# A graph layer on one core: another order of VectorE's operations, register loads a step ahead, and edge codes as products on TensorE

## The chip, the cores and the metric

One core of a Trainium2 chip runs the kernel. The metric is the device time of one execution in microseconds (us), lower is better. In what follows PE is TensorE (matrix products; PEld its weight loads), DVE is VectorE, ACT is ScalarE, POOL is GpSimd, and SP is the engine that issues most of the transfers. A small q behind an engine (DVEq) means its sequencer: register operations and the like, which are not counted as busy.

## The reference

There are 12500 nodes of 128 features and 400000 edges, sorted by their target `dst`. An edge's message is the source's row times one of two weight matrices, by the edge's type, plus a bias. Messages are summed by target; a third matrix is applied to the node itself; then relu, residual and a layer norm without gain:

```python
Xs = X[src]
m_data = Xs @ W_data.T + b_data
m_ctrl = Xs @ W_control.T + b_control
msg = jnp.where((edge_types == 0)[:, None], m_data, m_ctrl)
agg = jax.ops.segment_sum(msg, dst, num_segments=X.shape[0])
out = agg + (X @ W_self.T + b_self)
h = jax.nn.relu(out)
...
x = _layernorm(x + h, axis=-1)
```

## The kernel before

The sum over edges is taken first and the weights are applied after it: for each target and each type the kernel sums the rows of x, as three bf16 parts that add up to the f32 value (`x3`), and multiplies the sums by the weights afterwards. The sums run on PE: rows of messages times a 0/1 matrix which says to which target and type each edge goes.

Edges are cut into chunks of 128, and chunks into 25 groups of 125. A group has five windows of 25 chunks: 5 chunks ("p") whose rows POOL gathers from memory by indirect transfers (`msg`), and 20 chunks ("e") whose rows are fetched from a copy of x in on-chip memory by products with 0/1 matrices. In most groups the fifth window is gathered whole, so there are 109 "e" windows, and the main loop has 109 steps, `w`, one for each.

A step does several things for several windows at once. For window `w` PE picks rows (`got`, L974, with the matrix `pick`), ACT copies them to `emsg`, and PE adds them into `sums` (L803) with the 0/1 matrices `esel`, which DVE makes by comparing codes (L541, from `choose`). For the gathered chunks DVE makes `psel` (L541) in the same way. When a window is complete, DVE adds `sums` to the accumulator `acc` or `cnt` at a place known only from the data (`accumulate`, L860). That place is read from a table in on-chip memory into a register of DVE by `place_of` (`value_load`, L854), just before the addition that needs it.

For windows `w + 2` and `w + 3` DVE also works out where each edge's row lies and in which order (`give_slots`). Its operations, in short names with the page's tile names: `blocks` makes O (L541), `same` (L612), `tens` and the folds (L622, L627) add up O; PE turns these into counts (L634, in `before`); `ahead` (L642) adds them, `product` (L648) multiplies, `half` and `fourth` (L656), `eighth` (L661) and `found` (L666) reduce to a rank, `rank` (L671) copies it, `matrix` makes rm (L541), `key` (L678), `values` makes rv (L713). PE then puts the values in place (`put`, L726), ACT copies them to `cell`, SP writes them to memory and reads them back for all partitions (`spread`), and `pick_matrix` (L790) compares the result a step later. `over` and `own_before` (L686 to L701, L562, L568, L574) treat edges that found no room. The tile `prod` has one buffer, so `same` of window `w + 3` comes after `found` of `w + 2`. `sums` has two buffers.

Once for each group, `prep` turns the raw edge lists into codes: `begin`, `rows` (DVE: `rel`, `kind`, `code_r`, `worst`), `turn` (PE transposes into `side`, ACT copies), `then`. `finish_batch` (L1078 to L1124) applies the weights and the layer norm to finished rows.

What orders the work: each piece has a time within its step between 0 and 1, and `merged` sorts all pieces by that number into program order. A planner then orders each engine's queue by program order and by when it expects the operands. `after` (and `tc.issue_after`) binds an instruction to come later in the queue than another on the same engine. The list `order` in the main loop is such a chain for DVE: its pieces come one after another (`in_turn` hands each piece the instruction before it); work that is not on the list, such as the additions, `psel` and the norm, falls between where the planner puts it.

Of the kernel before, what the change touches and what calls it, by code (L numbers as in the profile page):

```python
# [8 lines left out]
FP = mybir.dt.float32  # L9
BF = mybir.dt.bfloat16  # L10
# [4 lines left out]
OP = mybir.AluOpType  # L15
# [4 lines left out]
P = 128  # L20
# [4 lines left out]
GC = 125  # L25
# [6 lines left out]
NE = 5  # L32
# [5 lines left out]
PW = DPC + 2 * PAD  # L38
EW = 86
AW = PW + DPC * (PL - 1)  # L40
WMAX = max(AW, EW)
CHUNKS = PB + EC
M0 = 50
R = 640
# [164 lines left out]
def short_path(ctx, tc, const, ident, eps, wT, brow, bad, x, src, dst, etype, ws, bs, out):  # L209
    nc = tc.nc  # L210
    keep = ctx.enter_context(tc.tile_pool(name="keep", bufs=1))
# [3 lines left out]
    pre = ctx.enter_context(tc.tile_pool(name="pre", bufs=2))  # L215
# [6 lines left out]
    def side():  # L222

        return ps1.tile([P, 512], FP, name="side")

    def windows(g):

        c = g * GC
        for i in range(NE):
            yield "p", i, c, PB  # L230
            yield "e", i, c + PB, EC
            c += PB + EC

    def sets(g):

        return NE if g % EACH == 0 else NE - 1
# [5 lines left out]
    each_e = [(g, i) for g in range(NG) for i in range(sets(g))]  # L242
    raw = {}
# [110 lines left out]
    ident_b = keep.tile([P, P], BF, name="ident_b")  # L354
# [39 lines left out]
    over_n = keep.tile([P, len(each_e)], BF, name="over_n")  # L394

    bounds_of, from_of, pick_first = row_tables(nc, keep, tmp)
    least = tmp.tile([1, NG, NWIN], FP, name="least")
    for i, (_, _, c, _) in enumerate(windows(0)):
        nc.vector.memset(least[:, :, i:i + 1], float(max(0, c * DPC - PAD)))
# [42 lines left out]
    def twice(t2, t):  # L442
        return nc.scalar.copy(t2, t.rearrange("p (n o) -> p n o", o=1).to_broadcast(list(t2.shape)))  # L443
# [35 lines left out]
    def prep(g):  # L479

        s, d, t = raw.pop(g)
        v = 0 if sets(g) == NE else 1
        width = bounds_of[:GC, v, 0:1]
        sf = pre.tile([GC, P], FP, name="sf", bufs=1)
        rel = pre.tile([GC, 2, P], BF, name="rel", bufs=1)
        code = pre.tile([GC, 2, P], FP, name="code_r", bufs=1)
        kind = pre.tile([GC, P], FP, name="kind_r", bufs=1)
        idx = pre.tile([P, GC], I32, name="idx_g", bufs=3)
        vals2 = pre.tile([P, GC, 2, 2], BF, name="vals2", bufs=3)
        near2 = pre.tile([P, GC, 2], BF, name="near2", bufs=3)  # L490

        def begin():
            nc.scalar.copy(sf, s)

        def rows():
            near = near_of(g, d)
            for k in range(2):
                nc.vector.tensor_scalar(rel[:, k], d, near[k], None, op0=OP.subtract)
            nc.vector.tensor_single_scalar(kind, t, 0.0, op=OP.not_equal)
            nc.vector.scalar_tensor_tensor(code[:, 1], kind, width, rel[:, 1], op0=OP.mult, op1=OP.add)  # L500
            nc.vector.scalar_tensor_tensor(code[:, 0], kind, float(PW), rel[:, 0], op0=OP.mult, op1=OP.add)
            for j, op in enumerate((OP.max, OP.min)):
                nc.vector.tensor_tensor(worst[:GC, v, j], worst[:GC, v, j], rel, op=op)

        def turn():
            ps = side()
            for k, each in enumerate((sf, code[:, 1], code[:, 0])):
                nc.tensor.transpose(ps[:, k * P:k * P + GC], each, ident[:GC, :GC])
            nc.scalar.copy(idx, ps[:, :GC])
            twice(vals2[:, :, 1, :], ps[:, P:P + GC])  # L510
            twice(near2, ps[:, 2 * P:2 * P + GC])

        def then():
            parts = pre.tile([P, 2, GC], I32, name="parts")
            nc.vector.tensor_single_scalar(parts[:, 0, :], idx, 7, op=OP.logical_shift_right)
            nc.vector.tensor_single_scalar(parts[:, 1, :], idx, 127, op=OP.bitwise_and)
            code_e = vals2.rearrange("p n v t -> p v t n")[:, 1, 0]
            pk = pre.tile([P, GC], FP, name="pk", bufs=3)
            nc.vector.scalar_tensor_tensor(pk, idx, 256.0, code_e, op0=OP.mult, op1=OP.add)
            blk = blks[g % 3]  # L520
            blk2 = pre.tile([P, GC, 2], BF, name="blk2", bufs=3)
            nc.scalar.copy(blk[:, :, EC:], parts[:, 0, :].rearrange("p (i c) -> p i c", c=CHUNKS)[:, :, PB:])
            twice(blk2, parts[:, 0, :])
            codes["e", g] = (blk, blk2, vals2, pk)
            codes["p", g] = (idx, near2)
            return twice(vals2[:, :, 0, :], parts[:, 1, :])

        return [begin, rows, turn, then]

    slots, placed = {}, []  # L530
    pairs = len(each_e)

    def after(ins):
        return tc.issue_after(ins.ins) if ins is not None else ExitStack()
# [252 lines left out]
    def pick_matrix(w, prev):  # L787
        t = slots[w]["pick"].rearrange("p j r -> p (j r)")
        with after(prev):
            return nc.vector.tensor_scalar(t, t, lane_f, None, op0=OP.is_equal)  # L790
# [55 lines left out]
    def acc_rows(g, a, b):  # L846
        begin_acc(g)
        return acc[g][:, a:b, :]

    def place_of(g, i):  # L850

        parts_in[g] = parts_in.get(g, 0) + 1
        with tc.issue_after(added[-2].ins) if len(added) > 1 else ExitStack():
            return nc.vector.value_load(raw["place"][0:1, g, i:i + 1], min_val=0, max_val=R - WMAX)  # L854

# [322 lines left out]
    def begin_slots(w):  # L1178
        slots[w] = give_slots(w)
        return list(slots[w]["begin"].values())  # L1180
# [25 lines left out]
    chunks, closed, rest = {}, {}, []  # L1206
# [22 lines left out]
    for w in range(pairs):  # L1229
        g, i = each_e[w]  # L1230
        more = [(0.5, lambda: later(near_rows))] if w == 0 else []
        first = 1 if g == 0 else 0
        if i == first and g + 1 < NG:
            prepared = [(at, lambda u=u: later(u)) for at, u in zip((0.15, 0.4, 0.65, 0.1), prep(g + 1))]
            more += prepared[:3]
        if i == first + 1 and g + 1 < NG:
            more += prepared[3:]
        if i == 3 and g + 2 < NG:
            load(g + 2)
        tiled, begin, chain, first = {}, [], {}, None  # L1240
        if w + 2 < pairs:
            tiled, first, chain = slots[w + 2]["tiled"], slots[w + 2]["before"], slots[w + 2]["chain"]
            begin = [(0.58, slots[w + 2]["over"])]
        elif w + 2 == pairs:
            tiled, begin = last_spares()
            first = begin.pop(0)[1]
        if w + 3 < pairs:
            more += [(0.503, lambda: begin_slots(w + 3))]
        if w + 1 == pairs:
            closes = [at for at, _ in chunks[w]][-1 - of_p(NG - 1, NE - 1)]  # L1250
            (xs, *most), (xs2, turn2, *last) = (finish(NG - 1, soon[i]) for i in (NE - 2, NE - 1))
            more += [(0.05, xs), (0.06, xs2), (0.98, turn2), (0.3, check_all)] + evenly(most, closes + 0.01, 0.97)
        units, ending, (second, third) = picked(w, tiled, ending, first)

        def started(name):
            return (lambda prev: slots[w + 3]["begin"][name](prev)) if w + 3 < pairs else None

        order = [
            (0.305, second), (0.31, chain.get("ahead")), (0.33, chain.get("product")), (0.34, chain.get("half")),
            (0.36, third), (0.38, chain.get("fourth")), (0.51, chain.get("eighth")),  # L1260
            (0.52, chain.get("found")), (0.53, started("same")), (0.54, chain.get("rank")),
            (0.55, chain.get("matrix")), (0.56, chain.get("key")), (0.57, chain.get("values")),
            (0.6, (lambda prev: pick_matrix(w + 1, prev)) if w + 1 < pairs else None),
            (0.62, started("blocks")), (0.64, started("tens")), (0.66, started("fold5")),
            (0.67, started("fold2")), (0.68, started("fold1")),
        ]
        order = [(at, f) for at, f in order if f]
        order = [(at, u) for (at, _), u in zip(order, in_turn([f for _, f in order]))]
        merged(
            chunks.pop(w, []),  # L1270
            units,
            begin,
            order,
            more,
            evenly(rest, 0.1),
        )
        slots.pop(w)
        rest = []
        for p in closed.pop(w, []):
            gp, ip = divmod(p, NE)  # L1280
            if ip == NE - 1:
                rest.append(lambda gp=gp: pass_on(gp))
                if gp < NG - 1:
                    rest += finish(gp, range(4))
                if gp + 2 < NG:
                    rest.append(lambda gp=gp: begin_acc(gp + 2))
# [143 lines left out]
```

## Time and profile before

| | before |
|---|---|
| median of 3 runs | 1719.48 us (1718.93 to 1721.28) |
| profiled execution, its own time | 1719.45 us |
| span in the profile | 1717.7 us |
| instructions | 67684 |
| granted TensorE clock, mean | 0.996 |
| DMA | 246.05 MB, mean 143 GB/s |

The span is the time from the program's first to its last instruction in the profile. The page gives busy time for each engine as a share of the span. Its chain follows the work that ended last backwards, at each step to what released it. "Issue" stands for time in which an engine waited for nothing that the profile shows. A row of the groups has line, engine, operation, output and inputs, then busy us, mean ns of one, and the idle time in front of them with what ended it.

### The profile page before, as it was taken

To read this page: it belongs to the slowest core of one execution; us is meant where nothing else is said; L and a number is where in the kernel's file an instruction comes from. 1 tells how busy PE (TensorE), PEld (TensorE's weight loads), DVE (VectorE), ACT (ScalarE), POOL (GpSimd) and SP (SyncE) were. 2 spreads that over 40 slices of the span, in tenths; PEclk is the share of its full clock that TensorE was granted. 3 is DMA by queue.
4 is the path that set the end of the run, shared out by engine and by line. 5 is a ranking of instruction groups with operands and counts; after the bars stand their busy time and mean duration, and the time that the engine had idled before them with its cause. 6 is when DMAs were issued, how large, how long until landed. Compare 5 with 4: busy or idle time off the path is not lost.

```text
span 1717.7 us, 67684 instructions
## 1 busy us (share of the span) xinstructions
PE 1554.5 (90%) x27966; PEld 1225.1 (71%) x27966; DVE 1577.5 (92%) x4078; ACT 1229.1 (72%) x2056; POOL 1217.5 (71%) x1022
## 2 busy tenths in 40 slices
PE   0699999899999999899899999999999999999998
PEld 0477777777777777777777777777777777777776
DVE  9799999999999999999999999999999999999994
ACT  7677767677767777677676777677686777677774
POOL 1377767777776777667777777677777787787682
PEclk9999999999999999999999999999999999999999
DMA  7944444444454444444444454444444454444442
GB/s 227 269 136 134 148 129 148 135 150 135 133 153 133 146 151 132 148 130 140 143 140 135 137 157 132 148 152 132 142 133 150 139 156 130 128 148 129 141 125 59
DMA packets 147605, 246.05 MB, mean 143 GB/s; under 512 B 35565, under 2 KB 114264, under 8 KB 147288
## 3 DMA queue, kind: packets, MB, share of 16 engines
q1 hardware_dynamic: 99128, 142.50, 24.9%
q0 software_dynamic: 48160, 99.14, 21.8%
q8 instruction: 221, 3.62, 0.8%
q14 instruction: 96, 0.79, 0.1%
HBM read 224.04 MB, written 17.52 MB: 141 GB/s over the span
## 4 chain that ended last, share of the span: by engine, by line
DVE 66%; PE 19%; issue 7%; ACT 3%; DVEq 3%; DMA 1%; SPq 0%; ACTq 0%
DVE esel L541 9%; PE sums L803 8%; DVE O L541 6%; DVE prod L656 6%; PE got L974 6%; DVE pick L790 5%; DVE prod L648 5%; DVE rv L713 4%; DVE psel L541 3%; DVE prod L627 3%; DVE prod L622 3%; DVE rm L541 2%; DVEq L854 2%; DVE found L666 2%; DVE prod L612 2%
## 5 line engine op out<-in xcount | busy, mean ns | idle before, releaser
L871 POOL DMA_INDIRECT msg<-rows,idx_g x945 | 1140.2, 1207 | 365.3 <-PE got L974 121.0
L988 ACT CAST emsg<-got 128x768 bf16<-128x768 f32 x1090 | 965.5, 929 | 305.0 <-PE got L974 291.2
L803 PE MATMUL sums<-esel,emsg 128*128 128x172 bf16 x7848 | 685.9, 238 | 7.9 <-DVE acc L860 7.8
L803 PEld LDWEIGHTS <-emsg 128*128 128x128 bf16 x7848 | 571.2, 98 | 118.8 <-issue 111.7
L974 PE MATMUL got<-x,pick 128*32 128x384 bf16 x10682 | 578.9, 330 | 9.8 <-ACT emsg L988 3.8
L974 PEld LDWEIGHTS <-pick 128*32 128x32 bf16 x10682 | 246.5, 96 | 138.3 <-issue 19.8
L541 DVE TENSOR_TENSOR esel<-code_col,code 128x1720 bf16<-128x1720 bf16 x327 | 293.5, 897 | 18.1 <-issue 12.9
L803 PE MATMUL sums<-psel,msg 128*128 128x48 bf16 x2835 | 161.4, 183 | 17.6 <-DVE acc L860 17.3
L803 PEld LDWEIGHTS <-msg 128*128 128x128 bf16 x2835 | 134.1, 97 | 26.2 <-issue 24.7
L648 DVE TENSOR_TENSOR prod<-O,ahead 128x2000 bf16<-128x2000 bf16 x109 | 130.9, 1201 | 9.9 <-DVE ahead L642 5.1
L656 DVE TENSOR_TENSOR prod<-prod 128x1200 bf16<-128x1200 bf16 x218 | 135.8, 623 | 3.0 <-DVE prod L648 0.2
L541 DVE TENSOR_TENSOR O<-cell_col,blk 128x2000 bf16<-128x2000 bf16 x109 | 129.7, 1190 | 0.5 <-ACT blk L443 0.5
L947 POOL DMA_INDIRECT both<-rows,idx x55 | 72.2, 1313 | 78.4 <-ACT emsg L988 37.1
L726 PE MATMUL side<-rv,O 128*128 128x64 bf16 x2180 | 84.8, 195 | 38.2 <-DVE rv L713 29.9
L790 DVE TENSOR_SCALAR pick<-pick,lane_f 128x3200 bf16<-128x3200 bf16 x109 | 112.5, 1033 | 1.5 <-DMA pick<-there 1.5
L726 PEld LDWEIGHTS <-O 128*128 128x128 bf16 x2180 | 81.0, 100 | 44.2 <-DVE rv L713 24.1
L541 DVE TENSOR_TENSOR psel<-near_col,near 128x1200 bf16<-128x1200 bf16 x125 | 96.4, 771 | 6.4 <-issue 6.3
L627 DVE TENSOR_TENSOR prod<-prod 128x500 bf16<-128x500 bf16 x327 | 94.1, 288 | 3.3 <-DVE prod L627 1.8
L713 DVE TENSOR_TENSOR rv<-rm,vals 128x1280 bf16<-128x1280 bf16 x109 | 89.5, 821 | 0.0
L622 DVE TENSOR_TENSOR prod<-O 128x1000 bf16<-128x1000 bf16 x109 | 72.9, 669 | 0.1
L860 DVE TENSOR_TENSOR acc<-acc,sums 128x172 f32 (+2 forms) x234 | 65.6, 280 | 6.3 <-PE got L974 1.6
L642 DVE TENSOR_REDUCE ahead<-side 128x100 bf16<-128x200 f32 x109 | 39.2, 360 | 30.0 <-PE side L634 27.8
(197 smaller groups left out, 1522.1 us busy)
## 6 DMA issues: line engine op xcount, KB each, us to landing
pick<-there SPq DMA_DIRECT2D x108, 800.0 KB
msg<-rows,idx_g POOLq DMA_INDIRECT x945
acc<-acc_start SPq DMA_DIRECT2D x23, 640.0 KB
rows<-x SPq DMA_DIRECT2D x6, 1344.0 KB
xs<-in_x_dram SPq DMA_DIRECT2D x99, 62.5 KB
out_dram<-h SPq DMA_DIRECT2D x99, 62.5 KB
xt<-in_x_dram SPq DMA_DIRECT2D x6, 896.0 KB
cnt<-cnt_start SPq DMA_DIRECT2D x22, 160.0 KB
```

The lines of the kernel that those rows point to most:

```text
L541: ins = nc.vector.tensor_tensor(sel.rearrange("p n (w t) -> p n w t", t=2), col[:rows].rearrange("p (o w t) -> p o w t", o=1, t=2).to_broa ...
L622: return nc.vector.tensor_add(h[:, :2 * CQ], s["O"][:, :2 * CQ], s["O"][:, 2 * CQ:])
L627: return nc.vector.tensor_add(h[:, to:to + n], h[:, a:a + n], h[:, b:b + n])
L648: return nc.vector.tensor_tensor(s["prod"][:, :, :NCELL], s["O"], s["ahead_b"].rearrange("p (o j) -> p o j", o=1).to_broadcast([P, EC, NCE ...
L656: return nc.vector.tensor_add(prod[:, :, :h], prod[:, :, :h], prod[:, :, h:2 * h])
L713: placed[:] = [nc.vector.tensor_tensor(rv.rearrange("p c v (r t) -> p c v r t", t=2), s["rm"].rearrange("p c (o r t) -> p c o r t", o=1, t ...
L726: nc.tensor.matmul(s["rk"][:m, :2 * CAP], s["held"][:, c * NCELL:c * NCELL + m], s["rv"][:, c].rearrange("p v r -> p (v r)"), start=(c == ...
L790: return nc.vector.tensor_scalar(t, t, lane_f, None, op0=OP.is_equal)
L803: last = nc.tensor.matmul(out, msg[:, j * D:(j + 1) * D], sel, start=(start and j == 0), stop=stop, skip_group_check=True)
L871: return nc.gpsimd.indirect_dma_start(out=msg, out_offset=None, in_=rows3[:, :], in_offset=bass.IndirectOffsetOnAxis(ap=codes["p", g][0][: ...
L974: last = nc.tensor.matmul(ps[CAP * a:CAP * (a + 1), :], slots[w]["pick"][:, a * NQ + q, :], x3[:, 4 * q + a - a0].rearrange("p j d -> p (j ...
L988: s["out"] = nc.scalar.copy(msg[:, :n], ps[:, :n, :3 * D])
```

## The change

Four edits. In `prep` the two f32 codes are no longer made on DVE and transposed; instead `rel` and `kind` (now bf16) go to PE, which turns and adds them as two bf16 products each, against the identity and a scaled identity (`type_step`, made once). A new `load_place` reads the places of the next step's windows one step ahead, the first behind `product`, the others behind `blocks`, and `place_of` returns them. `begin_slots`, which issues nothing, is called at 0.2. The list `order` gets new times and another sequence: `third` comes ahead of `half`, `rank` ahead of `same`, and `eighth` to `rank` move from about 0.51 to about 0.43.

```diff
+    type_step = keep.tile([P, 3, P], BF, name="type_step")
+    for v in range(2):
+        nc.vector.tensor_scalar(type_step[:, v], ident_b, bounds_of[:, v, 0:1], None, op0=OP.mult)
+    nc.vector.tensor_scalar(type_step[:, 2], ident_b, float(PW), None, op0=OP.mult)
...
-        code = pre.tile([GC, 2, P], FP, name="code_r", bufs=1)
-        kind = pre.tile([GC, P], FP, name="kind_r", bufs=1)
+        kind = pre.tile([GC, P], BF, name="kind_r", bufs=1)
...
             nc.vector.tensor_single_scalar(kind, t, 0.0, op=OP.not_equal)
-            nc.vector.scalar_tensor_tensor(code[:, 1], kind, width, rel[:, 1], op0=OP.mult, op1=OP.add)
-            nc.vector.scalar_tensor_tensor(code[:, 0], kind, float(PW), rel[:, 0], op0=OP.mult, op1=OP.add)
...
-            for k, each in enumerate((sf, code[:, 1], code[:, 0])):
-                nc.tensor.transpose(ps[:, k * P:k * P + GC], each, ident[:GC, :GC])
+            nc.tensor.transpose(ps[:, :GC], sf, ident[:GC, :GC])
+            for k, of in ((1, v), (0, 2)):
+                turned = ps[:, (2 - k) * P:(2 - k) * P + GC]
+                for j, (each, scale) in enumerate(((rel[:, k], ident_b), (kind, type_step[:, of]))):
+                    nc.tensor.matmul(
+                        turned, each, scale[:GC, :GC], start=(j == 0), stop=(j == 1), skip_group_check=True
+                    )
...
+    places = {}
+
+    def load_place(prev, w, k):
+
+        needed = [(gp, 2 * ip) for gp, ip in (divmod(p, NE) for p in closed.get(w, []))]
+        gp, ip = each_e[w - 1]
+        needed.append((gp, 2 * ip + 1))
+        for gp, ip in needed[k:] if k else needed[:1]:
+            with after(prev):
+                places[gp, ip] = nc.vector.value_load(
+                    raw["place"][0:1, gp, ip:ip + 1], min_val=0, max_val=R - WMAX
+                )
+        return prev
+
     def place_of(g, i):
 
         parts_in[g] = parts_in.get(g, 0) + 1
+        if (g, i) in places:
+            return places.pop((g, i))
...
         if w + 3 < pairs:
-            more += [(0.503, lambda: begin_slots(w + 3))]
+            more += [(0.2, lambda: begin_slots(w + 3))]
...
         order = [
-            (0.305, second), (0.31, chain.get("ahead")), (0.33, chain.get("product")), (0.34, chain.get("half")),
-            (0.36, third), (0.38, chain.get("fourth")), (0.51, chain.get("eighth")),
-            (0.52, chain.get("found")), (0.53, started("same")), (0.54, chain.get("rank")),
-            (0.55, chain.get("matrix")), (0.56, chain.get("key")), (0.57, chain.get("values")),
-            (0.6, (lambda prev: pick_matrix(w + 1, prev)) if w + 1 < pairs else None),
-            (0.62, started("blocks")), (0.64, started("tens")), (0.66, started("fold5")),
-            (0.67, started("fold2")), (0.68, started("fold1")),
+            (0.3, second),
+            (0.31, chain.get("ahead")),
+            (0.33, chain.get("product")),
+            (0.35, (lambda prev: load_place(prev, w + 1, 0)) if w + 1 < pairs else None),
+            (0.37, third),
+            (0.39, chain.get("half")),
+            (0.41, chain.get("fourth")),
+            (0.43, chain.get("eighth")),
+            (0.45, chain.get("found")),
+            (0.47, chain.get("rank")),
+            (0.49, started("same")),
+            (0.51, chain.get("matrix")),
+            (0.53, chain.get("key")),
+            (0.55, chain.get("values")),
+            (0.57, (lambda prev: pick_matrix(w + 1, prev)) if w + 1 < pairs else None),
+            (0.59, started("blocks")),
+            (0.61, (lambda prev: load_place(prev, w + 1, 1)) if w + 1 < pairs else None),
+            (0.63, started("tens")),
+            (0.65, started("fold5")),
+            (0.67, started("fold2")),
+            (0.69, started("fold1")),
         ]
```

More of the change, by code (lines that the diff above doesn't have):

```diff
@@ L482, in prep @@
         v = 0 if sets(g) == NE else 1
-        width = bounds_of[:GC, v, 0:1]
         sf = pre.tile([GC, P], FP, name="sf", bufs=1)
         rel = pre.tile([GC, 2, P], BF, name="rel", bufs=1)
-        code = pre.tile([GC, 2, P], FP, name="code_r", bufs=1)
-        kind = pre.tile([GC, P], FP, name="kind_r", bufs=1)
+        kind = pre.tile([GC, P], BF, name="kind_r", bufs=1)
         idx = pre.tile([P, GC], I32, name="idx_g", bufs=3)
```

## The prediction

> **What bounds the kernel now.** I read four views in this order: the page's sums and its chain, the busy time of the steady stretch, the waits of VectorE (DVE) and TensorE (PE), and then single instructions. First the page:
>
> ```profile
> PE 1554.5 (90%) x27966; PEld 1225.1 (71%) x27966; DVE 1577.5 (92%) x4078; ACT 1229.1 (72%) x2056; POOL 1217.5 (71%) x1022
> ...
> DVE 66%; PE 19%; issue 7%; ACT 3%; DVEq 3%; DMA 1%; SPq 0%; ACTq 0%
> ```
>
> DVE and PE are both near 90% busy, but the chain that ended last runs two thirds of its way over DVE; with DVEq (DVE's sequencer) and "issue" it is 66 + 3 + 7 = 76%. The steady stretch, without start and end:
>
> ```profile
> 100.00:1660.00 1560.00, 1459.22 (x26548) 1152.95 (x26536) 1460.60 (x3714) 1125.22 (x1906) 1168.52 (x963) 1.00 0.46 140
> ```
>
> The columns are the window, its length, then PE, PEld, DVE, ACT and POOL busy. DVE and PE idle about 100 us of 1560 each. Who waits for whom (total us, times, longest), DVE first, then PE:
>
> ```profile
> DVE ahead L642 <- PE side L634: 27.8, 45, 2.5
> DVE esel L541 <- issue: 12.9, 35, 0.9
> ...
> DVE psel L541 <- issue: 6.3, 13, 1.6
> ...
> DVE prod L648 <- DVE ahead L642: 5.1, 13, 0.7
> ...
> DVE cnt L840 <- issue: 4.6, 14, 0.5
> DVE parts L515 <- issue: 3.0, 7, 0.7
> ...
> DVE prod L648 <- issue: 2.3, 2, 1.2
> ...
> DVE pick L790 <- DMA pick<-there: 1.5, 2, 1.2
> ```
>
> ```profile
> PE side L574 <- DVE om_all L568: 31.6, 38, 1.6
> PE side L726 <- DVE rv L713: 29.9, 18, 13.0
> PE sums L803 <- DVE acc L860: 25.1, 39, 1.2
> PE side L634 <- DVE prod L627: 12.6, 14, 6.0
> ```
>
> DVE waits for PE at one place that counts, "ahead" (27.8 us). Most of its other waits are "issue": nothing the profile shows holds the instruction. PE's idle time is mostly waiting for DVE (31.6 + 29.9 + 25.1 + 12.6 = 99 us in these four rows, 13.0 of it in one wait). So DVE is the bound; PE is close behind it and tied to it both ways.
>
> The chain shows what "issue" is. Here are two pieces of it, and the register load by its line:
>
> ```profile
> 701.62 0.37 DVE ahead L642
> 701.98 0.76 DVEq L854
> 702.74 0.08 issue
> 702.81 0.19 DVEq L854
> 703.11 1.21 DVE prod L648
> ...
> 713.24 0.32 DVE prod L627
> ...
> 713.64 0.19 DVEq L854
> 713.94 0.13 DVE esel L541
> ```
>
> ```profile
> L854 DVEq TENSOR_LOAD <-place_i x234: 298/304/1396, 55.7 to 1705.0; - x117
> L854 DVEq FUSED_REGOPS  x234: 183/190/206, 56.9 to 1705.4; - x117
> ```
>
> L854 is the register load of a window's place. DVE's sequencer is busy with it, so the following DVE instruction isn't issued. At 713 the fold before it (L627) starts at 713.24 and "esel" only at 713.94: 0.70 us from start to start. A load therefore costs about 0.70 us less the duration of the instruction ahead of it, and nothing behind a long one.
>
> **The change part by part, in DVE time.**
>
> *Loads.* The six rows that end in "issue" or stand right behind "ahead" add up to 12.9 + 6.3 + 5.1 + 4.6 + 3.0 + 2.3 = 34.2 us in 84 waits. I put all of them down to loads, because each of the pieces looked at had L854 in it. After the change one load of a step stands behind "product" (L648) and the rest behind "blocks" (O):
>
> ```profile
> 705.65 0.47 DVE L656 TENSOR_TENSOR prod<-prod 128x600 bf16<-128x600 bf16 x1
> 706.15 0.30 DVE L661 TENSOR_TENSOR prod<-prod 128x280 bf16<-128x280 bf16 x1
> 706.37 1.04 DVE L541 TENSOR_TENSOR esel<-code_col,code 128x1720 bf16<-128x1720 bf16 x1
> ...
> 716.77 1.20 DVE L648 TENSOR_TENSOR prod<-O,ahead 128x2000 bf16<-128x2000 bf16 x1
> 718.01 0.78 DVE L656 TENSOR_TENSOR prod<-prod 128x1200 bf16<-128x1200 bf16 x1
> ```
>
> ```profile
> L541 DVE TENSOR_TENSOR O<-cell_col,blk 128x2000 bf16<-128x2000 bf16 x109 | 129.7, 1190 | 0.5 <-ACT blk L443 0.5
> ```
>
> Both covers (1.20 and 1.19 us) are longer than 0.70. From the loop's arithmetic (125 windows closed over 109 steps), 38 steps close two windows and so have two loads behind O: 2 x 0.69 = 1.38 us against 1.19 + 0.03, a stall of 0.16, 6 us in all. Each of the 84 waits also lost the overlap of the next instruction (0.08 us, next part), 7 us. Net: -34 - 7 + 6 = -35. The cover fails if the planner puts a short instruction between: behind one of 0.42 us the wait is 0.27 us, and 234 loads so placed would be 63 us, 29 more than now. Bounds -41 and +29; I take -35, since the edge is drawn to the long instruction itself.
>
> *Order.* In the rows above L661 needs what L656 wrote and starts 0.03 us after its end; the "esel" behind it needs nothing of it and starts 0.08 us before its end. So a dependent neighbour costs 0.11 us more. I count neighbours that depend on each other in the ten-odd pinned operations: before, ahead-product, product-half, fourth-eighth, eighth-found, found-same, rank-matrix, blocks-tens and three folds, ten; after, product-half, rank-matrix and found-same are parted, while half-fourth and found-rank come in: nine. One fewer is 109 x 0.11 = 12 us at most. Loose work already falls between some of them now, so the gain may be nil; I take the middle, -6. The waits on other engines that the new order may make are priced among the rivals.
>
> *The Trainium skill speaks against this term.* Its page "VectorE: DVE Perf Modes", section "The DRAIN you can't avoid", says the next operation doesn't start until the pipe has emptied; the order would then give 0, the sum below would be -46 and the time 1719 - 0.68 x 46 = 1688. The trace differs: "esel" at 706.37 began before L661 ended at 706.45. The page itself allows an earlier start to instructions that are not held.
>
> *Codes.* Per group of edges (25 of them) two operations leave DVE:
>
> ```profile
> 735.37 0.34 DVE L500 SCALAR_TENSOR_TENSOR code_r<-kind_r,bounds_of,rel 125x128 f32<-125x128 f32 x1
> 735.63 0.28 DVE L501 SCALAR_TENSOR_TENSOR code_r<-kind_r,rel 125x128 f32<-125x128 f32 x1
> 735.84 0.28 DVE L503 TENSOR_TENSOR worst<-worst,rel 125x256 bf16<-125x256 bf16 x1
> ```
>
> ```profile
> L384 DVE TENSOR_SCALAR ltri<-i,own_f 128x128 bf16<-128x128 int32 x4 | 0.9, 280 | 0.0
> ```
>
> From start to start they take 0.26 + 0.21 = 0.47 us, 11.8 us in 25 groups. The three new scaled identities at the start have the size of L384's (0.28 us): +0.8. "kind" in bf16 reads the same integers, so I count no change. Net -11. On PE each group loses two f32 transposes and gets four bf16 products:
>
> ```profile
> 805.54 1.28 PE L803 MATMUL sums<-esel,emsg 128*128 128x172 bf16 x15
> ...
> 806.65 0.59 PE L1078 MATMUL side<-ident,xs 125*128 125x125 f32 x4
> ```
>
> One more f32 transpose is worth at most 0.59 / 4 = 0.15 us and a bf16 product at most 1.28 / 15 = 0.085 us: +0.34 - 0.30, about 0.04 us, 1 us in 25 groups. It hides in PE's idle 100 us; without that cover it costs that 1 us. ACT's three copies of the result don't change, and no DMA or queue of SP or POOL is passed.
>
> *begin_slots at 0.2* only makes names. It issues no instruction and is counted at nothing; nothing need hide it.
>
> *Sum.* -35 - 6 - 11 = -52 us of DVE's queue, 0.48 us in each of 109 steps. Of that not all is time. The chain is 76% DVE's, which would pass 0.76 of it. From below: in 45 of 109 steps DVE already waits at "ahead" for PE, so what it saves before that place turns into more waiting there; 64 of 109 is 0.59. The middle, 0.68, gives -35 us. The profiled execution took 1719.45 us (span 1717.7), the median of the three runs is 1719.48. Forecast: 1719.45 - 35 = 1684 us. Own range: 52 x 0.59 to 52 x 0.85, 1675 to 1689, widened by the loads' and the order's unknowns (7 + 6) to 1668 to 1697.
>
> **The rivals.**
>
> *A: PE takes the bound.* PE is busy 1459 of 1560 us, as DVE is. If its modelled busy time is nearly all it can do, the "ahead" wait grows from 27.8 us by most of the gain. With a third of 52 passed: 1702. For it: 45 waits there already, and 90% in the page. Against: PE itself lists 99 us of waits for DVE, which shrink as DVE gets early.
>
> *B: PE has ample room, and all of it passes.* 1719 - 52 = 1667. For it: weight loads fill 71% of the span, far less than DVE's 92%, and the four rows of PE waiting for DVE. Against: the two engines' exchange within each step (L634 to "ahead", L568 to L574) has a fixed length. The Trainium skill, "Perfetto Trace Analysis", section "Identifying the Most-Contended Engine", calls matmul busy time a poor measure of PE's headroom and goes by weight loads; by that rule the time is B's. The trace's 45 waits at "ahead" speak for less.
>
> *C: slower; loose work comes late.* The chain from "eighth" to "values" moves from 0.51-0.57 to 0.43-0.55 and so ahead of loose DVE work of mid-step, above all the additions at L860 that free the two "sums" buffers. PE waits 25.1 us for them now, 39 times. If each step's addition comes behind "found", "rank" and "matrix", PE would stop for up to their 0.41 + 0.10 + 0.40 us:
>
> ```profile
> 707.34 0.48 DVE L666 TENSOR_REDUCE found<-prod 128x20 f32<-128x320 bf16 x1
> ...
> 708.20 0.17 DVE L671 CAST rank<-found 128x40 bf16<-128x40 f32 x1
> ...
> 708.44 0.47 DVE L541 TENSOR_TENSOR rm<-rank_col,rank 128x640 bf16<-128x640 bf16 x1
> ```
>
> Durations 0.48 + 0.17 + 0.47 = 1.1 us at most, less the overlap. It decides from 35 / 109 = 0.32 us a step on; at 0.45 us the time is 1719 + 49 - 35 = 1733. For it: a second "sums" buffer is all the slack there is. Against: the load of the place in front of these additions, which holds them back now, is gone.
>
> *D: no difference.* The loads' gaps lie where DVE would have waited for PE anyway, and PE's pace stays. Codes and loads then vanish into "ahead": 1719. Against: L854 is itself on the chain.
>
> POOL can't decide: its gathers are
>
> ```profile
> L871 POOL DMA_INDIRECT msg<-rows,idx_g x945 | 1140.2, 1207 | 365.3 <-PE got L974 121.0
> ```
>
> that is 1140.2 us busy and 365.3 idle before them, most of that waiting for PE, which it follows.
>
> **How the numbers follow.** Forecast (1675 to 1697) 0.45; A (1697 to 1715) 0.20; B (under 1675) 0.15; D (within 0.2%, 1716 to 1723, which is about what a measurement of this kernel can tell from no change) 0.07; C (over 1723) 0.13. Faster 0.45 + 0.20 + 0.15 = 0.80, same 0.07, slower 0.13. The range 1664 to 1714 leaves out C, D and the ends of A and B, some 2 in 10.
>
> **What would show it.** Right: "issue" waits in front of DVE's "esel", "psel" and "cnt" are down from 34 us to under 10; L854 starts directly after L648 and O; L500 and L501 are gone; DVE's queue per step is 0.4 us or more shorter, PE's waits for "om_all" and "acc" shrink, and "ahead" waits longer than 27.8 us but by less than 20. Wrong: "ahead" takes over 30 us more (A); PE's waits for "acc" at L803 double or more (C); the loads stand behind short instructions (the +29 us end); or "pick", now 0.03 of a step earlier, gets ahead of the transfer that it waited for only twice (1.5 us).

## The result and the profile after

The changed kernel took 1699.81 us (median, 1697.44 to 1701.05), the kernel before 1720.38 us on the same chip: a ratio of 0.9879 [0.9862, 0.9896], 20.6 us less. The forecast was 1684 us, range 1664 to 1714. The profiled execution took 1697.44 us, its span is 1695.7.

The page's sums and its chain, of the changed kernel:

```profile
PE 1549.3 (91%) x28016; PEld 1221.4 (72%) x28016; DVE 1561.0 (92%) x4031; ACT 1228.4 (72%) x2056; POOL 1242.9 (73%) x1022
...
DVE 47%; PE 31%; issue 9%; DMA 6%; ACT 4%; DVEq 3%; POOL 0%; SPq 0%; ACTq 0%; POOLq 0%
```

DVE is busy 16.5 us less (1577.5 before), the span is 22.0 us shorter, and the chain has moved from DVE (66% before) towards PE (19% before). But "issue" did not leave the chain: 7% before, 9% now. The waits of the changed kernel (us, times, longest), DVE's first, then PE's:

```profile
DVE ahead L647 <- PE side L639: 32.2, 36, 2.1
DVE prod L627 <- issue: 28.6, 44, 1.1
...
DVE esel L546 <- issue: 3.5, 8, 0.7
```

```profile
PE side L579 <- DVE om_all L573: 22.9, 29, 1.5
PE sums L808 <- DVE acc L881: 18.7, 32, 1.4
```

The scattered "issue" waits of before (esel 12.9, psel 6.3, cnt 4.6 and others) are nearly gone. In their place is one that was not there: 28.6 us in 44 waits in front of "tens" (L627), the operation behind the new place of the loads. PE's waits for "om_all" (31.6 before) and "acc" (25.1) shrank, "ahead" grew from 27.8 to 32.2.

What stands between "blocks" and "tens" shows the cause. DVE's instructions of the changed kernel (start, duration, line, operation; in brackets the idle time in front), and the load in the same stretch:

```profile
745.94 1.18 DVE L546 TENSOR_TENSOR O<-cell_col,blk 128x2000 bf16<-128x2000 bf16 x1
747.04 0.22 DVE L696 TENSOR_SCALAR full<-top 128x16 f32<-128x16 f32 x1
747.18 0.16 DVE L700 CAST top_i<-top 128x16 int32<-128x16 f32 x1
747.30 0.17 DVE L698 TENSOR_REDUCE over_n<-full 128x2 bf16<-128x16 f32 x1
747.38 0.17 DVE L702 TENSOR_SCALAR bits<-top_i 128x16 int32<-128x16 int32 x1
...
747.54 0.17 DVE L706 TENSOR_SCALAR bits<-top_i 128x16 int32<-128x16 int32 x1
748.07 0.68 DVE L627 TENSOR_TENSOR prod<-O 128x1000 bf16<-128x1000 bf16 x1 [0.37 <-issue]
```

```profile
L864 DVEq TENSOR_LOAD <-place_i x1: 302/302/302, 747.4 to 747.4; - x1
```

The load does not run inside O's 1.18 us, as the prediction had it. It starts at 747.4, 1.4 us after O, when the small operations of `over`, which work on one another's results, have been released; "tens" comes 0.7 us after it, and for 0.37 of that DVE has nothing to do. Counted over the trace, all 44 stalls are of this kind: 25 steps with one load behind O stall for 0.36 us each, 19 steps with two for 1.03 us, 9.0 + 19.6 us.

### The profile page after: what moved, and what is told of

Same layout as the page of the kernel before. It is cut to its first block, busy times and chain, and to the rows that moved or that the text cites. A ratio compares the mean times of both kernels' runs of the same rounds, so it can differ in the third digit from the quotient of the medians.

```text
span 1695.7 us, 67734 instructions
## 1 busy us (share of the span) xinstructions
PE 1549.3 (91%) x28016; PEld 1221.4 (72%) x28016; DVE 1561.0 (92%) x4031; ACT 1228.4 (72%) x2056; POOL 1242.9 (73%) x1022
## 4 chain that ended last, share of the span: by engine, by line
DVE 47%; PE 31%; issue 9%; DMA 6%; ACT 4%; DVEq 3%; POOL 0%; SPq 0%; ACTq 0%; POOLq 0%
PE sums L808 13%; PE got L995 10%; DVE esel L546 7%; DVE O L546 5%; DVE pick L795 4%; DVE prod L661 4%; PE side L1116 3%; DVE prod L632 3%; DVE rv L718 3%; DVEq L864 3%; DMA pick<-there 2%; DVE prod L627 2%; ACT emsg L1009 2%; DVE found L671 2%; DVE rm L546 2%
## 5 line engine op out<-in xcount | busy, mean ns | idle before, releaser
L892 POOL DMA_INDIRECT msg<-rows,idx_g x945 | 1161.7, 1229 | 330.3 <-issue 122.6
L968 POOL DMA_INDIRECT both<-rows,idx x55 | 76.0, 1382 | 66.0 <-ACT emsg L1009 30.3
L627 DVE TENSOR_TENSOR prod<-O 128x1000 bf16<-128x1000 bf16 x109 | 73.9, 678 | 30.0 <-issue 28.6
L647 DVE TENSOR_REDUCE ahead<-side 128x100 bf16<-128x200 f32 x109 | 39.1, 359 | 32.8 <-PE side L639 32.2
L881 DVE TENSOR_TENSOR acc<-acc,sums 128x172 f32 (+2 forms) x234 | 65.6, 280 | 3.5 <-PE sums L808 2.9
```

The source lines that it names most:

```text
L627: return nc.vector.tensor_add(h[:, :2 * CQ], s["O"][:, :2 * CQ], s["O"][:, 2 * CQ:])
L892: return nc.gpsimd.indirect_dma_start(out=msg, out_offset=None, in_=rows3[:, :], in_offset=bass.IndirectOffsetOnAxis(ap=codes["p", g][0][: ...
```

## The experiments

On some chips the kernel before took 1941 to 1965 us, against 1720 on the others. There the other engines wait longer for PE: with the loads alone, the first experiment, three rows of DVE's "ahead" add up to 37.2 + 33.1 + 10.8 = 81 us, against one of 26.4 on a faster chip, at a mean granted clock of 0.973 against 0.992. The chain there:

```profile
PE 64%; ACT 15%; DVE 9%; issue 7%; another core or an unknown queue 2%; DMA 1%; DVEq 0%; ACTq 0%; SPq 0%
```

They are called chips with late PE below; why they differ is not known. A ratio holds for its own chip, and the chip's time of the kernel before stands beside each. The changed kernel itself was measured on a chip of 1720 us only, and the expectations were written for such chips, so they are decided only by the runs there.

**Loads alone.** The old list, with the two loads put behind "product" and "blocks" (and `load_place` itself):

```diff
-            (0.305, second), (0.31, chain.get("ahead")), (0.33, chain.get("product")), (0.34, chain.get("half")),
+            (0.305, second), (0.31, chain.get("ahead")), (0.33, chain.get("product")),
+            (0.335, (lambda prev: load_place(prev, w + 1, 0)) if w + 1 < pairs else None), (0.34, chain.get("half")),
...
-            (0.62, started("blocks")), (0.64, started("tens")), (0.66, started("fold5")),
+            (0.62, started("blocks")),
+            (0.63, (lambda prev: load_place(prev, w + 1, 1)) if w + 1 < pairs else None), (0.64, started("tens")), (0.66, started("fold5")),
```

> Only the register loads are moved a step ahead; order and codes stay as before. Theory 1 (the loads were mis-sized: those behind O stand behind the short operations of 'over' and still stop VectorE): the waits 'issue' on VectorE fall only from 34 us to some 25, most of them now in front of 'tens', and the time falls by 5 to 12 us, to about 1711. Theory 2 (the loads' stalls are gone as forecast and TensorE took the gain): 'issue' waits in front of 'tens' under 10 us, 'ahead' waits up by 15 us or more, time about 1706. The forecast's own term: 35 us x 0.68 = 24 us less, 1696.

> The same kernel as e1_loads_only, for a chip on which the kernel before takes about 1720. Theory 1: the loads' stalls fall by about 12 us only, most of what is left stands in front of 'tens', 1707 to 1714. Theory 2: stalls gone, gain lost elsewhere, 1706 with 'ahead' waits up by 15 us. The forecast's term: 1696.

Measured: 0.9748 [0.973, 0.9766], 1675.65 us beside 1719.75: 44 us less, more than the whole change gives and below every time expected. On a chip where PE is late: 1.0034 [1.0003, 1.0064], 1951.06 beside 1942.11. Of the faster run, the page, DVE's waits and PE's, then DVE's instructions at the same place in the step and the load there:

```profile
PE 1553.0 (93%) x27966; PEld 1222.9 (73%) x27966; DVE 1570.0 (94%) x4078; ACT 1224.1 (73%) x2056; POOL 1239.0 (74%) x1022
...
DVE 42%; PE 40%; issue 6%; ACT 5%; DMA 4%; DVEq 1%; POOL 0%; SPq 0%; ACTq 0%; POOLq 0%
```

```profile
DVE ahead L642 <- PE side L634: 26.4, 37, 2.1
...
DVE acc L876 <- PE sums L803: 4.9, 6, 1.2
```

```profile
PE side L574 <- DVE om_all L568: 15.4, 18, 1.0
PE sums L803 <- DVE acc L876: 12.7, 29, 1.0
```

```profile
738.37 0.18 DVE L691 TENSOR_SCALAR full<-top 128x16 f32<-128x16 f32 x1
738.44 0.17 DVE L695 CAST top_i<-top 128x16 int32<-128x16 f32 x1
738.52 1.19 DVE L541 TENSOR_TENSOR O<-cell_col,blk 128x2000 bf16<-128x2000 bf16 x1
739.63 0.16 DVE L693 TENSOR_REDUCE over_n<-full 128x2 bf16<-128x16 f32 x1
739.71 0.16 DVE L697 TENSOR_SCALAR bits<-top_i 128x16 int32<-128x16 int32 x1
...
739.94 0.67 DVE L622 TENSOR_TENSOR prod<-O 128x1000 bf16<-128x1000 bf16 x1
```

```profile
L859 DVEq TENSOR_LOAD <-place_i x1: 308/308/308, 738.7 to 738.7; - x1
```

Here `over` (0.58) precedes "pick" (0.60), so "full" and "top_i" are done before O. The four small operations stand between O and "tens" as well, but their operands are there, and the load starts 0.14 us into O; "tens" follows without a gap, 1.42 us after O's start against 2.13 in the changed kernel. The changed list has "pick" at 0.57, ahead of `over`, and so the whole run of small operations falls between O and the load. The trace shows what the load waits for. In both kernels there are 44 steps in which loads and these small operations come between O and "tens", and in all of them the first load starts 0.050 to 0.054 us after the end of "top_i": ahead of O with the loads alone (738.44 + 0.17), behind it in the changed kernel (747.18 + 0.16). With the loads alone three of these steps stall, for 0.33 us each. That the load stands in the queue behind the first "bits", which needs "top_i", is inferred from this; the trace doesn't give the queue's order. PE's waits for "om_all" and "acc" fell by 16 and 12 us, so by these rows the loads had delayed PE.

**Loads and codes, old order.** The changed kernel with the list of the experiment above and `begin_slots` back at 0.503.

```diff
-            more += [(0.2, lambda: begin_slots(w + 3))]
+            more += [(0.503, lambda: begin_slots(w + 3))]
...
-            (0.3, second),
-            (0.31, chain.get("ahead")),
-            (0.33, chain.get("product")),
-            (0.35, (lambda prev: load_place(prev, w + 1, 0)) if w + 1 < pairs else None),
-            (0.37, third),
...
+            (0.305, second), (0.31, chain.get("ahead")), (0.33, chain.get("product")),
+            (0.335, (lambda prev: load_place(prev, w + 1, 0)) if w + 1 < pairs else None), (0.34, chain.get("half")),
+            (0.36, third), (0.38, chain.get("fourth")), (0.51, chain.get("eighth")),
...
```

> The changed kernel with the old list (old sequence and times, the two loads in it behind 'product' and 'blocks', begin_slots at 0.503): loads and codes without the new order. Theory 3 (the loads alone are worth 44 us, as e1_loads_only_2 had it; the new order gives 25 us back, because in it 'over' comes after 'pick' and the loads behind O wait for its chain): no 'issue' in front of 'tens', and VectorE's queue is another 11 us shorter than in e1_loads_only_2: 1664 to 1672. Theory 4 (the codes on TensorE are what costs, not the order): 1685 to 1700, slower than e1_loads_only_2.

> The same kernel as e7_loads_codes (loads and codes, old order), for a chip on which the kernel before takes about 1720. Theory 3 (the new order costs the changed kernel some 25 us, the codes are a small gain): 1664 to 1672. Theory 4 (the codes cost, the order is harmless): 1685 to 1700. If codes and order share the 24 us between the changed kernel and e1_loads_only_2: about 1680 to 1685.

> Loads and codes in the old order once more, for a chip on which the kernel before takes about 1720; there the expectation is that of e7_loads_codes_2: 1664 to 1672 if the new order is what costs the changed kernel 25 us, 1685 to 1700 if the codes are.

Measured: 0.9739 [0.9724, 0.9754], 1676.4 us beside 1720.76, 4 us above the range expected of a costly order and 9 below that of costly codes. Where PE is late: 1.0018 [0.9992, 1.0044] beside 1964.71 and 1.0009 [0.9984, 1.0035] beside 1962.55. Two things follow. The codes are worth no difference that shows (0.9739 against 0.9748). And the new order, which with `begin_slots` (it issues nothing) is all that lies between this kernel and the changed one, costs (0.9879 - 0.9739) x 1720 = 24 us; from the two intervals, some 4 us either way. Its page (on the chip of 1720 us), DVE's waits and PE's:

```profile
PE 1558.5 (93%) x28016; PEld 1230.0 (73%) x28016; DVE 1559.7 (93%) x4031; ACT 1223.7 (73%) x2056; POOL 1236.6 (74%) x1022
...
PE 43%; DVE 38%; ACT 6%; issue 6%; DMA 5%; DVEq 1%; POOL 0%; SPq 0%; ACTq 0%; POOLq 0%
```

```profile
DVE ahead L647 <- PE side L639: 33.0, 38, 2.7
...
DVE esel L546 <- PE sums L808: 8.6, 5, 4.1
DVE acc L881 <- PE sums L808: 8.2, 8, 3.0
```

```profile
PE sums L808 <- ACT last L1053: 9.3, 4, 3.8
```

DVE is busy 10.3 us less than with the loads alone (1559.7 against 1570.0), as the codes promised; "ahead" waits 6.6 us longer, "acc" 3.3 and "esel" (3.8 with the loads alone) 4.8 longer for PE, 14.7 together. By these rows what the codes saved went into waits for PE, which leads the chain by now; the profiled execution of this kernel was the longest of its five (1680.47 us), so some of the 14.7 may be this execution's own.

**Codes alone, and order alone** (the changed kernel without the loads and the new list; the kernel before with the new list and `begin_slots` at 0.2):

```diff
-            (0.305, second), (0.31, chain.get("ahead")), (0.33, chain.get("product")), (0.34, chain.get("half")),
...
+            (0.3, second),
+            (0.31, chain.get("ahead")),
+            (0.33, chain.get("product")),
+            (0.37, third),
...
```

> Only the codes as products on TensorE; loads and order as before. Both theories: VectorE's queue loses 11 us. Theory 1 (VectorE is the bound and passes 0.7 of what it saves): 8 us less, 1712. Theory 2 (TensorE close behind, 0.4 passed): 4 us less, 1716.

> Only the new sequence and times of the list, without load_place, codes as before. Theory 1: what is left of the measured 20.6 us after loads (8) and codes (8), some 4 us less, 1716; a change of up to 12 us of VectorE's queue would be 1712. Theory 2: the same or slower, 1719 to 1725, since work off the list comes later and TensorE waits more for 'acc'.

Both fell on a chip with late PE (before 1942.11): codes 1.0026 [1.0007, 1.0046], order 1.0088 [1.0053, 1.0123]. On these chips the kernels with the old order came out 0.1 to 0.3% slower, those with the new order 0.9 to 2.1%. Neither was measured alone on a chip of 1720 us.

**Loads put elsewhere.** In the changed kernel, one load each behind "product", "values" and "pick", so that none has `over` in front of it:

```diff
-        for gp, ip in needed[k:] if k else needed[:1]:
+        for gp, ip in needed[k:k + 1]:
...
+            (0.56, (lambda prev: load_place(prev, w + 1, 1)) if w + 1 < pairs else None),
...
+            (0.575, (lambda prev: load_place(prev, w + 1, 2)) if w + 1 < pairs else None),
             (0.59, started("blocks")),
-            (0.61, (lambda prev: load_place(prev, w + 1, 1)) if w + 1 < pairs else None),
```

> The changed kernel with its loads set apart: the first behind 'product' as now, the second behind 'values', the third behind 'pick', none behind O. Theory 1: the 28.6 us of 'issue' in front of 'tens' go, VectorE is still the bound, 0.7 of it passes: 20 us less than the changed kernel, 1680. Theory 2: TensorE is the bound already; 'ahead' waits grow by 20 us and the time stays within 6 us of the changed kernel, 1694 to 1700.

> The same kernel as e4_loads_apart, for a chip on which the kernel before takes about 1720. Theory 1 (the loads behind O still stop VectorE, which is the bound: one more operation of 0.41 us a step cost 54 us against the changed kernel): the 28.6 us of 'issue' in front of 'tens' go and the time is 20 to 30 us under the changed kernel, 1670 to 1680. Theory 2 (TensorE, or the gathers of GpSimd, whose mean went from 1207 to 1229 and 1298 ns, bind as soon as VectorE gains): within 6 us of the changed kernel, 1694 or more, with longer waits at 'ahead'.

Measured: 0.9855 [0.983, 0.9879], 1695.22 us beside 1719.75; with late PE 1.0211 [1.0178, 1.0245]. The 28.6 us in front of "tens" are gone from DVE's waits, but the time is only some 4 us below the changed kernel's, some 5 us either way by the two intervals, which is no difference clear of noise. The load stall is therefore not the whole price of the new order: without it, this kernel is still (0.9855 - 0.9739) x 1720 = 20 us behind the old order, again some 5 us either way. Its waits (DVE, PE, ACT) show what came instead:

```profile
DVE ahead L647 <- PE side L639: 43.6, 44, 2.8
DVE acc L881 <- PE sums L808: 20.8, 12, 4.7
```

```profile
PE sums L808 <- ACT last L1053: 23.4, 8, 5.3
```

```profile
ACT last L1053 <- DMA both<-rows,idx: 39.5, 14, 6.7
```

Read it from below: ACT waits for the spare rows ("both"), which POOL gathers; PE waits for ACT's copy of them; DVE waits for PE's sums. The same ACT row is not in the waits of the kernel before, is 12.3 us in the changed kernel, 9.0 with the loads alone and 17.6 with loads and codes, so it is not the new order's alone. POOL's gathers have come late.

**`over` earlier.** In the changed kernel, so that "full" and "top_i" precede "pick" again:

```diff
-            begin = [(0.58, slots[w + 2]["over"])]
+            begin = [(0.56, slots[w + 2]["over"])]
```

> The changed kernel with one number changed: 'over' of the window two steps ahead at 0.56 and no longer 0.58, so that it comes before 'pick' as in the kernel before. The loads, the sequence of the list and the codes stay. Theory 3: the 28.6 us of 'issue' in front of 'tens' fall under 5, since 'full' and 'top_i' have run before O and nothing behind O waits; 20 to 28 us less than the changed kernel, 1672 to 1680. Theory 5 (the stall goes but the new order has another price, as e4_loads_apart_2 suggests, where 28 us of stalls went and 5 us of time): 1690 to 1697, with 'ahead' waits over 40 us.

> The same kernel as e8_over_early ('over' at 0.56, all else as changed), for a chip on which the kernel before takes about 1720. Theory 3 (the late 'over' is what the new order costs: its chain stands between O and the loads): no 'issue' in front of 'tens' and 1672 to 1682, as the old order with loads and codes (1676). Theory 6 (the new sequence of the long operations itself costs, through GpSimd: 43 gathers over 2 us in the changed kernel and 53 in e4_loads_apart_2 against 16 to 21 in the old order): 'issue' gone, 40 or more gathers over 2 us, their mean over 1250 ns, 1690 to 1698.

It fell on a chip with late PE both times: 1.0124 [1.0083, 1.0165] and 1.0127 [1.0106, 1.0149]. The stall in front of "tens" was gone there too, and the kernel was still 1.2 and 1.3% slower than the one before; loads and codes in the old order, beside the same 1964.71 us as the first of these, were 0.2% slower. Whether this edit mends the changed kernel on a chip of 1720 us is open.

**One more DVE operation in each step.** In the changed kernel, another comparison of rm's size (0.41 us in the queue, 107 times, 44 us) that nothing needs:

```diff
+    junk = keep.tile([P, EC, CAP], BF, name="junk")
...
+            (0.52, (lambda prev: select(junk, rank_col, slots[w + 2]["rank"], prev)[1]) if w + 2 < pairs else None),
```

> The changed kernel with one operation more on VectorE in each step that has a window two steps ahead: 'matrix' (rm) is made a second time into a tile that nothing reads. It takes 0.41 us from start to start in 107 steps, 44 us of VectorE's queue. Theory 1 (VectorE is the bound and passes 0.7): about 30 us more than the changed kernel, 1730 where the changed kernel takes 1700. Theory 2 (TensorE is the bound after the change): under 10 us more. On a chip on which TensorE is the slower one, as in the runs of the four kernels before, both expect under 10 us.

Measured: 1.02 [1.017, 1.0231], 1753.78 us beside 1720.9, which is 54 us over the changed kernel. So more work on DVE does cost time, as it would with DVE the bound, and more than the 30 us expected of it. It costs more than its 44 us, and POOL's rows offer a reason. The gathers "msg" (945 of them) and "both" (55) in the changed kernel, with the loads alone, with the loads elsewhere, and in this run; busy us, mean ns, then the idle time in front:

```profile
L892 POOL DMA_INDIRECT msg<-rows,idx_g x945 | 1161.7, 1229 | 330.3 <-issue 122.6 <-PE got L995 94.7 <-PE sums L808 60.6
L968 POOL DMA_INDIRECT both<-rows,idx x55 | 76.0, 1382 | 66.0 <-ACT emsg L1009 30.3 <-DVE esel L546 26.6 <-issue 7.9
```

```profile
L887 POOL DMA_INDIRECT msg<-rows,idx_g x945 | 1168.8, 1237 | 312.2 <-issue 125.8 <-PE got L990 76.7 <-PE sums L803 65.5
L963 POOL DMA_INDIRECT both<-rows,idx x55 | 65.1, 1184 | 65.5 <-DMA srcs<-in_src_dram 26.3 <-ACT emsg L1004 18.4 <-ACT idx L591 9.6
```

```profile
L892 POOL DMA_INDIRECT msg<-rows,idx_g x945 | 1189.2, 1258 | 308.0 <-issue 118.3 <-PE sums L808 63.6 <-PE got L995 63.3
L968 POOL DMA_INDIRECT both<-rows,idx x55 | 80.2, 1458 | 58.3 <-DVE prod L666 25.7 <-ACT emsg L1009 22.4 <-issue 8.4
```

```profile
L892 POOL DMA_INDIRECT msg<-rows,idx_g x945 | 1226.7, 1298 | 314.8 <-issue 138.4 <-PE got L995 71.5 <-PE sums L808 63.1
L968 POOL DMA_INDIRECT both<-rows,idx x55 | 83.3, 1515 | 62.5 <-DVE prod L666 27.6 <-ACT emsg L1009 21.9 <-issue 8.8
```

POOL does nothing new in any of these, yet a gather's mean rises from 1207 ns before to 1298, and that of "both" from 1313 to 1515 in the new order, while it falls to 1184 in the old. In this run 945 x (1298 - 1229) ns = 65 us of POOL's time came with 44 us of DVE's; the two causes can't be parted here. ACT waits 43.4 us for "both" in this run, against 12.3 in the changed kernel.

## Why the prediction came out as it did

In time, the forecast was 24 us from the loads, 4 from the order and 7 from the codes, 35 in all; the runs give 44, -24 and none that shows, 20 in all. The total fell into the range because errors of opposite sign cancelled; that is luck, not the working.

*Loads, term mis-sized.* Forecast -35 us of DVE, 0.68 of it passed, 24 us; measured 44 alone. Two things were missing. The pass-through was too low: with the additions free of their loads PE too stopped waiting ("om_all" and "acc", 28 us less), and "ahead" did not grow (26.4), so DVE's gain was not given back there. And 44 us (40 to 46 by its interval) is at least the whole of the bound of -41, and more than the 34.2 us of waits that the trace of before shows; where the rest comes from is open. The share of 0.85 that bounded the range from below had no row behind it, and the loads went beyond it.

*Loads' cover, the warning that came true.* The prediction named "a short instruction between" as the way in which the cover fails, and dismissed it because the edge is drawn to the long instruction. The edge binds the load to come after O; it does not keep the queue's other work from coming in between. 28.6 us in 44 waits is this; a step with two loads behind O was priced at 0.16 us, and 19 of them took 1.03. The sign to look for ("esel", "psel" and "cnt" under 10 us) was met all the same, as the wait had moved to a row that was not on the list. What was not foreseen is the condition. Short operations in between do no harm when they are ready (loads alone), and do when one of them still waits for its neighbour (changed list). Of the other signs of being wrong, "pick" did get ahead of its transfer more often, 5.7 us in 8 waits, but it waits 4.4 us with the loads alone as well.

*Order, step failed, wrong sign.* I counted dependent neighbours, -12 to 0, and took -6. That counts what an operation costs its neighbour and leaves out what the new sequence does to the work that falls between: `over` against "pick", with the load behind both, and, by the rows on POOL, perhaps its gathers. The rivals carried the danger of slower, but in the wrong place: C expected PE to wait for the additions (L860, now L881), and that wait fell from 25.1 to 18.7 us.

*Codes, right in DVE's time, wrong in the sum.* Loads and codes together show DVE 10.3 us less busy, against 11 forecast, and nothing in the time: by the rows above PE was the next bound behind the larger gain of the loads. That is A's mechanism, applied to this term alone; for the changed kernel A itself does not hold, as "ahead" grew by 4.4 us and not by over 30.

*"POOL can't decide", not tenable.* The idle time of 365.3 us before the gathers was read as slack, most of it waiting for PE. The rows of the kernel before:

```profile
L871 POOL DMA_INDIRECT msg<-rows,idx_g x945 | 1140.2, 1207 | 365.3 <-PE got L974 121.0 <-issue 117.3 <-PE sums L803 98.3
L947 POOL DMA_INDIRECT both<-rows,idx x55 | 72.2, 1313 | 78.4 <-ACT emsg L988 37.1 <-DVE found L666 26.4 <-issue 8.3
```

In every trace there are at least 0.30 us between one gather and the next, and in 882 of 999 places before, 939 in the changed kernel and 967 with the loads alone no more than 0.35 us, whatever the rows name as having ended them. So 945 x 0.30 = 284 us of the 365.3 are a fixed pause and not slack. What is left is 82 us before, 47 in the changed kernel, 29 with the loads alone and 25 with the loads elsewhere: POOL, 71 to 75% busy by the page, has hardly any idle time once the loads are out of DVE's way. Its own need by the rows, 945 x (mean + 0.30) + 55 x (mean of "both" + 0.30), is 1424 + 89 = 1513 us before, 1534 with the loads alone, 1537 in the changed kernel and 1472 + 97 = 1569 with the loads elsewhere. In the last POOL's lateness reaches DVE through ACT and PE, row by row above. In the changed kernel it is small (12.3 us at ACT, 3.3 at PE), and its need only 3 us above that with the loads alone.

*What stays open* is the order's other 20 us, those that stayed when the stall went. Longer gathers fit this: with the loads elsewhere POOL needs 35 us more than with the loads alone in the old order. But they were not tested by themselves, the chain gives POOL only 1% there, and in the changed kernel, where the stall is, they add next to nothing. Here is a long one in the changed kernel (POOL, then DVE at that time):

```profile
520.14 0.95 POOL L892 DMA_INDIRECT msg<-rows,idx_g  x1 [0.30 <-issue]
521.39 3.26 POOL L892 DMA_INDIRECT msg<-rows,idx_g  x1 [0.30 <-PE sums L808]
```

```profile
520.86 0.81 DVE L718 TENSOR_TENSOR rv<-rm,vals 128x1280 bf16<-128x1280 bf16 x1
521.60 1.04 DVE L795 TENSOR_SCALAR pick<-pick,lane_f 128x3200 bf16<-128x3200 bf16 x1
522.56 0.17 DVE L691 MAX8 top<-key 128x8 f32<-128x20 f32 x1
522.65 1.17 DVE L546 TENSOR_TENSOR O<-cell_col,blk 128x2000 bf16<-128x2000 bf16 x1
523.86 0.68 DVE L627 TENSOR_TENSOR prod<-O 128x1000 bf16<-128x1000 bf16 x1
524.46 0.23 DVE L881 TENSOR_TENSOR acc<-acc,sums 128x80 f32 x1
```

The gather takes 3.26 us instead of 0.95 and ends 0.1 us after "tens" (523.86 + 0.68). Counted over the trace, 16 gathers take over 2 us before, 22 with the loads alone and 17 with loads and codes, but 44 in the changed kernel and 53 with the loads elsewhere. The new list puts "values", "pick", "blocks" and "tens" end to end, where the old one left "pick" apart. Stretches of over 2 us in which bf16 operations of 0.5 us and more follow one another on DVE, each starting before the one ahead ends, number 60 to 69 in the three kernels with the old order, 118 in the changed one and 134 with the loads elsewhere. The count hangs on what is called a break: if pauses of up to 0.1 us are allowed within a stretch, there are 207 to 215 in all five. This is a weak association: no run held the order fixed and changed only the length of these stretches.

The Trainium skill, "SBUF — State Buffer", section "Who interferes with whom", says that VectorE and GpSimd share a port pair under an exclusive lock, so that some VectorE operations keep GpSimd out while they run. A gather of 3.26 us beside one of 0.95 would fit that, but no run here shows it: of the operations in the stretch above only "pick" (1.04 us) is of a kind that the section lets take the whole pair; the other large ones are tensor_tensor, which by it stand only in the way of GpSimd's reads.

## What to carry to other kernels

Look at what stands between a register load and the long instruction that is to hide it, in the order in which the queue runs: ready work in between is harmless, work that waits for its neighbour uncovers the load. Test the parts of a change apart even when the total comes out as forecast; here one part gave 44 us and another took 24 of it back, and the version without the new order (1676 us, 0.974 of the time before) beats both kernels on the chips of 1720 us. Look at more than one chip: where PE is late that version gains nothing (1.001 and 1.002). When one engine's stalls are removed, read the idle time of the others for fixed pauses before calling it slack (here 284 of 365 us), and expect later terms to be worth less than the first.

## What the runs showed of the hardware that was not expected

A register load on DVE's sequencer can start long before operations that lie between it and the one it was bound to: with the loads alone 0.14 us into O's 1.19 us, before the four small operations that the trace shows between O and "tens". In the changed kernel it started 1.4 us after O, and the next operation behind it 0.7 us later. In all 44 steps of either kernel it came 0.050 to 0.054 us after the end of "top_i", so by this it passes operations whose operands are there and is held by one that still waits (that it stands behind them in the queue is inferred). Most loads take 0.30 us, a few much longer, up to 1.44:

```profile
L864 DVEq TENSOR_LOAD <-place_i x233: 296/304/1443, 60.6 to 1657.0; - x117
```

Two gathers of 128 rows, one after the other, took 0.95 and 3.26 us, with nothing on POOL's own queue between them but the pause of 0.30 us. That pause stands between all of the 1000 gathers of every trace; the page's busy share leaves it out.
